# Layer 0 of a two-layer vision state-space model: input projection with 128-row and paired 64-row matmuls, norm sums partly added on GpSimd, residual taken from the gate's tile, new list order

## The chip, the cores and the metric

The kernel runs on one core of a Trainium2 chip. The metric is the device time of one execution in microseconds. Matrix products run on TensorE (PE; PEld is its weight load), elementwise work on VectorE (DVE), ScalarE (ACT) and GpSimd (POOL); every DMA is issued by SyncE (SP). Everything is in fp32.

## What is computed

The input `x` is (4, 128, 128, 192), channels last. Both layers have the form norm, block, residual. The change lies in layer 0, which for each image computes:

- a group norm statistic of x over groups of 6 channels; it is not applied to x but folded into the weights: each row of the projection's weight is multiplied by the channel's inverse deviation, and the mean is turned into a bias.
- `xz = x @ Win.T`: 192 channels to 2 x 384. The first 384 are `xi`, the last 384 the gate `z`.
- `xs = silu(conv3x3(xi) + b)`, depthwise, over 384 channels.
- `x_dbl = x_proj_w @ xs` gives 12 channels for the step size, one row B and one row C; `delta = softplus(dt_w @ dts + dt_b)`.
- a scan over all 16384 pixels, state size 1: `h = exp(delta * A) * h + delta * B * xs`.
- three depthwise 3x3 convolutions of the map of h with dilations 1, 3 and 5, edges replicated, weighted by alpha and summed: `h_f`.
- `y = h_f * C + xs * D`; a layer norm of y over its 384 channels (mean, then the mean of the squared differences); times `silu(z)`; `out = y @ Wout.T`, back to 192 channels.
- residual: `x1 = x + out`, and the norm statistic of x1 for layer 1.

Layer 1 (four scan directions with 16 states, joint processing of image pairs) and the final output follow; the change leaves them as they are.

## The kernel before

Before layer 0, `transpose_in` turns x from pixels-first to channels-first with PE transposes and writes it to a scratch tensor `xT`, as 2 x 96 channels by pixels; on the way it takes the statistics, which `gn_finish` turns into mean and inverse deviation (`gn0`, 96 partitions by two halves).

Layer 0 works on chunks of T = 1024 pixels (R = 8 rows of the picture), NCH = 16 chunks for each of four images, 64 in all. The 384 inner channels are NB = 3 blocks of 128 partitions. For each chunk:

- `load_xa` loads 9 rows of xT into a tile of 96 partitions x 2 halves.
- `project_in` (L392) makes one block of xi: for each half chunk h of 512 pixels it accumulates two matmuls, s = 0 and 1, each with 96 rows of channels. ACT adds the bias and copies to `xi` with a border (L407).
- `conv_in` makes nine products on ACT (L447) and adds eight of them on POOL (L452), then silu (L454); the result xs stays in SBUF and also goes to HBM (`xsd`).
- `project_x` (L471) and `scan`: PE makes the step sizes (L496) and spreads B over partitions (L483), ACT computes softplus and exp (L529, L532), POOL multiplies (L534), DVE multiplies and scans (L537, L539), ACT copies h to a padded tile (L546), POOL fills the pads (L507, L510), SP stores it to HBM (`hpad`).
- one chunk later, `half` for each half chunk: for each block `item` loads shifted copies of h (`sa`, 96 partitions: three rows of taps for 32 channels), runs the dilated taps on PE with diagonal weights (L574), adds eight near taps on DVE (L595), and combines with C, D and xs into y (L605, L606).
- then the layer norm. PE averages over channels with a 128x128 matrix of 1/384 (L633), three accumulating matmuls, one for each block; DVE subtracts (L639), ACT squares (L641), PE averages the squares in the same way (L633), ACT takes log and exp (L644, L646), DVE scales (L653).
- the gate: `xz` is a load of x for these 512 pixels (L648); PE projects it (L660), ACT takes silu (L666), DVE multiplies (L669). PE projects back to 192 channels (L677).
- the residual: x is loaded once more, in two tiles `xr` of 96 partitions (L686), DVE adds PE's result (L688) and takes statistics (L690), SP stores each to `x1T` (L692).

The order of the instructions on each engine is written by a planner in the kernel. The class `Order` collects operations with an engine, a cost, what they read and write, and a due time. `emit` then picks, again and again, the operation that can start first; among those that can start within `idle` of an engine's being free it takes the one of the lowest rank. The rank is the place in the program minus `early`, and an ACT operation that needs another activation table than the one loaded has `keep` added. The result is one fixed list for each engine, SP's DMA issues included: at run time each engine goes through its list in order, and an operation that waits holds up all behind it. A buffer `Buf` has a tag and a number of copies; its next use waits for the last reader of the one before.

Where the weights come from: `scaled(part, b)` scales the projection weights for image b out of a resident tile `win` of both parts on DVE, and computes the bias with small matmuls (L356). Part 0 is xi's, part 1 the gate's; each scaled tile has one copy.

Of the kernel before, what the change touches and what calls it, by code (L numbers as in the profile page):

```python
# [10 lines left out]
F32 = mybir.dt.float32  # L11
# [189 lines left out]
class Maker:  # L201
# [23 lines left out]
    def transpose_in(self, x, xT, gn, ident, p96, eps):  # L225
        nc, tc = self.nc, self.tc
        with tc.tile_pool(name="t_sb", bufs=3) as sb, tc.tile_pool(
            name="t_st", bufs=2
        ) as stp, tc.tile_pool(name="t_ps", bufs=3, space=PSUM) as ps:
            for b in range(B):  # L230
# [26 lines left out]
                self.gn_finish(stp, g, stats, p96, eps, gn[:, b])  # L257

    def layer0(self, xT, x1T, hpad, xsd, gn_in, gn_out, w, ident, p96, eps):
# [8 lines left out]
        with ctx:  # L270
# [6 lines left out]
            win = cp.tile([HC, 2, 6 * 128], F32, name="win")  # L277
            nc.sync.dma_start(win, w["win0"].rearrange("(s c) e -> c s e", s=2))
# [15 lines left out]
            nc.vector.memset(avg, 1.0 / (NB * 128))  # L294

# [30 lines left out]
            od = Order()  # L326
# [13 lines left out]
            def scaled(part, b):  # L340


                t, o = buf(f"w{part}", 1, HC, 2, NB * 128), buf(f"b{part}", 2, 128, NB)
                g = bank2("AC"[part])

                def scale():
                    for s in range(2):
                        nc.vector.tensor_scalar(
                            t()[:, s], win[:, s, part * NB * 128 : (part + 1) * NB * 128],
                            gn_in[:, b, s, 1:2], None, ALU.mult,  # L350
                        )

                def means():
                    for k in range(NB):
                        for s in range(2):
                            nc.tensor.matmul(  # L356
                                g()[:, 0, k : k + 1], t()[:, s, k * 128 : k * 128 + 128],
                                gn_in[:, b, s, 0:1], start=(s == 0), stop=(s == 1),
                            )

                op("DVE", 0.8, scale, writes=[t])
                op("PE", 1.5, means, reads=[t], writes=[g], early=258)
# [6 lines left out]
            def load_xa(b, j):  # L369
# [3 lines left out]
                t = buf("xa", 2, HC, 2, R + 1, W)  # L373
                op("SP", 0.6, lambda: nc.sync.dma_start(
                    t()[:, :, n0 : n0 + hi - lo + 1].rearrange("c s r w -> c s (r w)"),
                    xT[b][:, :, lo * W : (hi + 1) * W].rearrange("s c t -> c s t"),
                ), writes=[t], size=786e3)
                xa[b, j] = t
# [3 lines left out]
            def project_in(b, j, k):  # L382

                x, wt, bt = xa[b, j], wxz[0], bias[0]
# [3 lines left out]
                def mm():  # L388
                    for h in range(2):
# [1272 lines left out]
```

## Time and profile before

Three runs took 26333.76, 26409.49 and 26457.49 us; the median is 26409.49 us.

| | us |
|---|---|
| profiled execution | 26512.26 |
| its span | 26510.5 |
| PE busy | 24193.3 (91%) |
| DVE busy | 21935.4 (83%) |
| ACT busy | 21016.8 (79%) |
| POOL busy | 19902.8 (75%) |
| mean granted TensorE clock | 0.940 |

By stage, the span divides into: transposing in, 0 to 375 us; layer 0, 375 to 6120 us; the input of layer 1, 6120 to 7950 us; its scans, 7950 to 24800 us; the output, 24800 to 26510 us. So layer 0 is 5745 us, 22% of the span, 90 us for each of its 64 chunks.

How to read the lines that follow. Each group of instructions has the line in the kernel, the engine, the operation, what it writes and reads with tile sizes (partitions x elements), the count, and after the bar the busy time in us and the mean in ns; then the idle time of that engine just before these instructions, and what ended it. Busy times of PE are modelled at their ends, since matmuls are pipelined. The clock is the share of full speed that was granted to TensorE. The DMA share is the mean share of time in which the core's 16 DMA engines had a packet; it can go a little above 1 where packets overlap.

### The profile page before, as it was taken

The page shows a single profiled execution, that of the slowest core. Times are in us where ns is not written, and L with a number is a line of the kernel's source. Part 1 is how long each engine was busy: PE and PEld are TensorE (multiplying, and loading weights), DVE is VectorE, ACT ScalarE, POOL GpSimd, SP SyncE. Part 2 cuts the span into 40 slices and gives each one's busy share as a digit, 9 for nine tenths or more (in the row PEclk, how much of TensorE's full clock was granted, in tenths as well). Part 3 has the DMA queues.
Part 4 walks back from the last instruction along what each step waited for, and adds up shares of the span by engine and source line. Part 5 has one row for each costly group of instructions (what it writes and reads, how often), then busy time and mean ns, then how long its engine had stood idle before and what let it go on. Part 6 is the DMA issues. An engine that isn't in the chain of part 4 may idle for free.

```text
span 26510.5 us, 438073 instructions
## 1 busy us (share of the span) xinstructions
PE 24193.3 (91%) x169220; PEld 9017.9 (34%) x169220; DVE 21935.4 (83%) x15401; ACT 21016.8 (79%) x24359; POOL 19902.8 (75%) x9450
## 2 busy tenths in 40 slices
PE   5999999998799999999999999999999999999699
PEld 3333333332233333333333333333333333333255
DVE  4888888888788889989898888888898888988643
ACT  5988898985588888888888888888888888888433
POOL 3777777763488888888888888888888888888400
PEclk7999999998899999999999899999899999999799
DMA  7999999995544444444444444444444444444573
GB/s 213 242 239 241 242 239 241 239 241 182 185 130 127 133 130 136 135 128 125 117 126 134 126 135 130 130 130 130 125 136 131 117 123 115 133 130 130 182 236 105
DMA packets 1667058, 4220.17 MB, mean 159 GB/s; under 512 B 238545, under 2 KB 387473, under 8 KB 1661905
## 3 DMA queue, kind: packets, MB, share of 16 engines
q1 hardware_dynamic: 1664976, 4192.14, 58.0%
q8 instruction: 1340, 21.95, 0.4%
q14 instruction: 742, 6.07, 0.1%
HBM read 3252.11 MB, written 939.10 MB: 158 GB/s over the span
## 4 chain that ended last, share of the span: by engine, by line
PE 40%; DVE 18%; ACT 11%; issue 6%; DMA 4%; POOL 3%; SPq 0%; DVEq 0%; POOLq 0%; ACTq 0%
DVE h L1207 14%; PE f L1174 13%; PE Y L1221 11%; ACT h L1185 6%; PE s L1028 3%; ACT dA L1201 3%; POOL hc L1213 2%; PE s L1051 2%; DMA C<-cs 2%; PE z L785 1%; PE hf L574 1%; DVE D L1100 1%; DVE acc L896 1%; PE f L785 1%; PE s L1094 1%
## 5 line engine op out<-in xcount | busy, mean ns | idle before, releaser
L1213 POOL TENSOR_TENSOR hc<-h,C 128x1024 f32<-128x1024 f32 x6144 | 14335.4, 2362 | 2412.5 <-PE Y L1221 1154.9
L1207 DVE TENSOR_TENSOR_SCAN h<-dA,st,h 128x1024 f32<-128x1024 f32 x5760 | 13130.9, 2331 | 779.9 <-ACT st L1237 290.6
L1185 ACT COPY h<-f 128x1024 f32<-128x1024 f32 (+3 forms) x8192 | 6332.9, 799 | 2256.1 <-PE f L1174 2185.0
L1174 PE MATMUL f<-D,dT 32*64 32x256 f32 x98304 | 7167.9, 408 | 777.5 <-ACT h L1185 633.6
L1221 PE MATMUL Y<-hc,sel 128*64 128x512 f32 x24576 | 7001.5, 657 | 475.1 <-POOL hc L1213 219.9
L1201 ACT ACTIVATE dA<-d,alog 128x1024 f32<-128x1024 f32 x6144 | 6905.9, 1124 | 301.6 <-DVE h L1207 247.2
L1174 PEld LDWEIGHTS f<-D,dT 32*64 32x64 f32 x98304 | 3279.1, 138 | 6688.2 <-ACT h L1185 4815.8
L452 POOL TENSOR_TENSOR xs<-xs,pr 128x1024 f32<-128x1024 f32 x1536 | 3637.3, 2371 | 329.2 <-ACT pr L447 249.4
L595 DVE SCALAR_TENSOR_TENSOR hf<-hh,vec,hf 128x512 f32<-128x512 f32 x3072 | 2317.8, 755 | 412.9 <-PE hf L574 272.7
L1221 PEld LDWEIGHTS Y<-hc,sel 128*64 128x64 f32 x24576 | 1322.6, 141 | 2979.6 <-issue 1811.3
L574 PE MATMUL hf<-sa,diag 96*32 96x512 f32 x18432 | 2152.3, 600 | 13.2 <-DMA sa<-hpad 11.3
L447 ACT ACTIVATE pr<-xi,vec 128x1024 f32<-128x1024 f32 x1536 | 1713.8, 1143 | 301.1 <-POOL xs L452 296.0
L1100 DVE TENSOR_TENSOR D<-s,mask 128x1024 f32<-128x1024 f32 x1024 | 1238.3, 1209 | 842.0 <-PE s L1094 842.0
L534 POOL TENSOR_TENSOR dl<-dl,xs 128x1024 f32<-128x1024 f32 x192 | 454.7, 2368 | 830.6 <-ACT dA L532 735.5
L574 PEld LDWEIGHTS hf<-sa,diag 96*32 96x32 f32 x18432 | 561.9, 109 | 1479.3 <-issue 1390.5
L1061 POOL TENSOR_TENSOR u<-l,u 128x1024 f32<-128x1024 f32 x384 | 907.2, 2363 | 163.4 <-ACT l L1054 136.0
L1207 DVE TENSOR_TENSOR_SCAN h<-dA,h 128x1024 f32<-128x1024 f32 x384 | 857.1, 2274 | 78.5 <-ACT dA L1201 45.3
L1051 PE MATMUL s<-pj,w 128*128 128x512 f32 x1536 | 892.3, 664 | 7.0 <-ACT l L1054 2.8
L1028 PE MATMUL s<-u,w 128*128 128x512 f32 x1536 | 756.4, 630 | 53.3 <-DMA prev<-xc 52.6
L1054 ACT ACTIVATE l<-s,vec 128x512 f32<-128x512 f32 x768 | 527.8, 687 | 328.5 <-PE s L1051 323.9
L1094 PEld LDWEIGHTS s<-ident,pj 128*128 128x128 f32 x4096 | 554.1, 196 | 599.5 <-issue 256.7
L392 PE MATMUL f<-xa,w 96*128 96x512 f32 (+1 forms) x1536 | 724.8, 616 | 25.7 <-ACT xi L407 25.5
(202 smaller groups left out, 21859.5 us busy)
## 6 DMA issues: line engine op xcount, KB each, us to landing
C<-cs SPq DMA_DIRECT2D x4096, 256.0 KB, 4.7
sa<-hpad SPq DMA_DIRECT2D x2304, 276.0 KB, 7.1
d<-delta SPq DMA_DIRECT2D x1536, 256.0 KB, 4.1
u<-xc SPq DMA_DIRECT2D x384, 512.0 KB, 4.6
delta<-l SPq DMA_DIRECT2D x384, 512.0 KB, 3.6
y<-y SPq DMA_DIRECT2D x1536, 128.0 KB, 3.2
hh<-hpad SPq DMA_DIRECT2D x384, 414.0 KB, 7.7
hpad<-hp SPq DMA_DIRECT2D x192, 552.0 KB, 7.2
```

The lines of the kernel that those rows point to most:

```text
L447: op("ACT", 1.1, lambda pr=pr, t=t: nc.scalar.activation(rows(pr()), x()[:, t // 3 : t // 3 + R, t % 3 : t % 3 + W], AF.Copy, scale=v(k, V ...
L452: op("POOL", 2.38, lambda pr=pr: nc.gpsimd.tensor_tensor(o(), o(), pr(), ALU.add), reads=[pr], writes=[o], early=-429)
L574: nc.tensor.matmul(o()[32 * g : 32 * g + 32], diag[:, d, s, k, g], x[:, g, :, c0 : c0 + W], start=(d == 0 and s == 0), stop=(d == 1 and s ...
L595: nc.vector.scalar_tensor_tensor(o3, hh()[:, 1 + dy : 5 + dy, PAD + dx : PAD + dx + W], v(k, V0_K + col), o3, ALU.mult, ALU.add,)
L1028: nc.tensor.matmul(g(), wt()[:, 0, i], uu[i]()[:, 512 * c : 512 * c + 512], start=(i == 0), stop=(i == 2),)
L1100: nc.vector.tensor_tensor(t().rearrange("t a (n s) -> t (a n) s", s=32), g()[:, : 2 * NS].unsqueeze(2).to_broadcast([128, 2 * NS, 32]), ma ...
L1174: nc.tensor.matmul(gs()[64 * jn : 64 * jn + 64, n, 256 * a : 256 * a + 256], td()[rt, r // 64, 2 * sb + a], tD()[rt, a, 256 * jn : 256 * j ...
L1185: nc.scalar.copy(H[:, at : at + nq, 256 * sb : 256 * sb + 256].rearrange("p q (a r s) -> p q a r s", a=2, s=32)[:, :, :, 2 * rp : 2 * rp + 2],
L1201: op("ACT", 1.16, lambda: nc.scalar.activation(a(), d(), AF.Exp, scale=alog[:, c : c + 1]), reads=[d], writes=[a], table="exp", early=-522)
L1207: nc.vector.tensor_tensor_scan(hs[:, way], a()[:, way], hs[:, way], 0.0 if at == 0 else s0()[:, q : q + 1], ALU.mult, ALU.add,)
L1213: op("POOL", 2.4, lambda: nc.gpsimd.tensor_tensor(t(), hs, tC(), ALU.mult), reads=[hq, tC], writes=[t])
L1221: nc.tensor.matmul(ym()[64 * th : 64 * th + 64], sel, t()[:, 512 * th : 512 * th + 512], start=(q == 0), stop=(q == NQ - 1),)
```

## The change

Seven things change, all in layer 0 or just before it:

- The input projection's tile. `load_xa` now loads channels 0 to 127 into `xa` (128 partitions, 9 rows) and channels 128 to 191 into `xb`, whose partitions 0 to 63 hold the first half chunk's rows and partitions 64 to 127 the second's: three DMAs where there was one. `project_in` issues s = 0 for both half chunks with 128 rows, then s = 1 with 64 rows, half 0 in rows 0 to 63 and half 1 in rows 64 to 127.
- For that, part 0 of the weights is laid out with channels 128 to 191 twice. The resident `win` goes; `scaled` loads the raw weights from HBM for every image into the scaled tile and scales them in place.
- The norm's values go to HBM (`gn0d`) at the end of each image of `transpose_in`, and are loaded again as `gn128` in the new layout ahead of layer 0.
- The layer norm's sums. Before each average, POOL adds the three blocks (two adds of 128 x 512), and PE averages the sum with one matmul where there were three.
- The residual is added in the gate's tile `xz`, which gets two copies; the second load of x and the tiles `xr` go. One store writes both halves to `x1T`.
- The planner gets `keep=428, idle=0.150` (before 20 and 0.3) and other values of `early` nearly everywhere in layer 0, so that the fixed lists have another order.
- The costs given to the planner follow: 2.75 for `project_in` (3.6), 0.92 for an average (2.65), 1.22 for an add on POOL.

The diff, without the other changes of `early`:

```diff
-    def transpose_in(self, x, xT, gn, ident, p96, eps):
+    def transpose_in(self, x, xT, gn, gnd, ident, p96, eps):
...
                 self.gn_finish(stp, g, stats, p96, eps, gn[:, b])
+                nc.sync.dma_start(gnd[b].rearrange("(s c) v -> c s v", s=2), gn[:, b])
...
-            win = cp.tile([HC, 2, 6 * 128], F32, name="win")
-            nc.sync.dma_start(win, w["win0"].rearrange("(s c) e -> c s e", s=2))
...
+            gn128 = cp.tile([128, B, 2, 2], F32, name="gn128")
+            for b in range(B):
+                nc.sync.dma_start(gn128[:, b, 0], gnd[b][:128])
+                for q in range(2):
+                    nc.sync.dma_start(gn128[64 * q : 64 * q + 64, b, 1], gnd[b][128:])
...
-            od = Order()
+            od = Order(keep=428, idle=0.150)
...
+                if part:
+                    t = buf("w1", 1, HC, 2, NB * 128)
+                    gn = [(slice(0, HC), gn_in[:, b, s]) for s in range(2)]
+                    rows_ = [(slice(0, HC), s, src[s * HC : (s + 1) * HC]) for s in range(2)]
+                else:
+                    t = buf("w0", 1, 128, 2, NB * 128)
+                    gn = [(slice(0, 128), gn128[:, b, 0]), (slice(0, 128), gn128[:, b, 1])]
+                    rows_ = [
+                        (slice(0, 128), 0, src[:128]),
+                        (slice(0, 64), 1, src[128:]),
+                        (slice(64, 128), 1, src[128:]),
+                    ]
+
+                def load():
+                    for p, s, x in rows_:
+                        nc.sync.dma_start(t()[p, s], x)
...
+                op("SP", 0.5, load, writes=[t], size=295e3, early=75)
...
-                t = buf("xa", 2, HC, 2, R + 1, W)
-                op("SP", 0.6, lambda: nc.sync.dma_start(
-                    t()[:, :, n0 : n0 + hi - lo + 1].rearrange("c s r w -> c s (r w)"),
-                    xT[b][:, :, lo * W : (hi + 1) * W].rearrange("s c t -> c s t"),
-                ), writes=[t], size=786e3)
+                t, t2 = buf("xa", 2, 128, R + 1, W), buf("xb", 2, 128, 5, W)
+                x = xT[b].rearrange("s c t -> (s c) t")
+
+                def load():
+                    for p, ch, at, n, r in (
+                        (slice(0, 128), slice(0, 128), n0, hi - lo + 1, lo),
+                        (slice(0, 64), slice(128, C), n0, 5 - n0, lo),
+                        (slice(64, 128), slice(128, C), 1, hi - R * j - 4, R * j + 5),
+                    ):
...
                 def mm():
-                    for h in range(2):
-                        m = min(4, n - 4 * h)
-                        for s in range(2):
+                    for s in range(2):
+                        for h in range(2):
+                            m = min(4, n - 4 * h)
+                            p = slice(64 * h, 64 * h + 64) if s else slice(0, 128)
                             nc.tensor.matmul(
-                                g()[:, h, : m * W], wt()[:, s, k * 128 : k * 128 + 128],
-                                x()[:, s, 1 + 4 * h : 1 + 4 * h + m],
+                                g()[:, h, : m * W], wt()[p, s, k * 128 : k * 128 + 128],
+                                x2()[p, 1 : 1 + m] if s else x()[:, 1 + 4 * h : 1 + 4 * h + m],
                                 start=(s == 0), stop=(s == 1),
                             )
...
-                op("PE", 3.6, mm, reads=[x, wt], writes=[g, t], early=219)
-                op("POOL", 0.3, edges, writes=[t])
-                op("ACT", 1.12, copy, reads=[g, bt], writes=[t], early=-657)
+                op("PE", 2.75, mm, reads=[x, x2, wt], writes=[g, t], early=-48)
+                op("POOL", 0.3, edges, writes=[t], early=2409)
+                op("ACT", 1.12, copy, reads=[g, bt], writes=[t], early=-21)
...
-                gm, gv, xz = bank(), bank(), buf("xz", 1, HC, 2, 512)
+                gm, gv, xz = bank(), bank(), buf("xz", 2, HC, 2, 512)
+                ysum = buf("ys", 1, 128, 512)
...
                 def average(out, src):
-                    for k in range(NB):
-                        nc.tensor.matmul(
-                            out(), avg, src[k](), start=(k == 0), stop=(k == NB - 1)
-                        )
-
-                op("PE", 2.65, lambda: average(gm, ys), reads=ys, writes=[gm], early=-411)
+                    nc.tensor.matmul(out(), avg, src(), start=True, stop=True)
+
+                def add(out, a, b):
+                    op("POOL", 1.22, lambda: nc.gpsimd.tensor_tensor(out(), a(), b(), ALU.add),
+                       reads=[a, b], writes=[out])
+
+                add(ysum, ys[0], ys[1])
+                add(ysum, ysum, ys[2])
+                op("PE", 0.92, lambda: average(gm, ysum), reads=[ysum], writes=[gm])
...
-                op("PE", 2.65, lambda: average(gv, sq), reads=sq, writes=[gv], early=-411)
+                add(sq[0], sq[0], sq[1])
+                add(sq[0], sq[0], sq[2])
+                op("PE", 0.92, lambda: average(gv, sq[0]), reads=[sq[0]], writes=[gv])
...
-                    xr = buf(f"xr{s}", 1, HC, 512)
-                    op("SP", 0.4, lambda s=s, xr=xr: nc.sync.dma_start(
-                        xr(), xT[b][s, :, c1 : c1 + 512]), writes=[xr], size=197e3)
-                    op("DVE", 0.68, lambda s=s, xr=xr: nc.vector.tensor_tensor(
-                        xr(), xr(), g()[:HC, s], ALU.add), reads=[g], writes=[xr])
+                    op("DVE", 0.68, lambda s=s: nc.vector.tensor_tensor(
+                        xz()[:, s], xz()[:, s], g()[:HC, s], ALU.add), reads=[g], writes=[xz], early=-120)
...
-                    op("SP", 0.4, lambda s=s, xr=xr: nc.sync.dma_start(
-                        x1T[b][s * HC : (s + 1) * HC, c1 : c1 + 512], xr()
-                    ), reads=[xr], size=197e3)
+                op("SP", 0.4, lambda: nc.sync.dma_start(
+                    x1T[b][:, c1 : c1 + 512].rearrange("(s c) t -> c s t", s=2), xz()
+                ), reads=[xz], size=393e3)
```

## The prediction

> **What bounds the kernel now.** The edit touches layer 0, the short work before it, and nothing later. I therefore read first the busy time by stage (columns: window, its length, then busy us and instruction counts of PE, PE weight loads, DVE, ACT, POOL; granted clock; DMA share; GB/s).
>
> ```profile
> 375.00:570.00 195.00, 103.31 (x228) 38.68 (x232) 26.57 (x27) 155.01 (x162) 172.98 (x105) 0.61 0.31 90
> 570.00:5870.00 5300.00, 5263.00 (x26004) 1761.30 (x26000) 4375.11 (x5636) 4741.76 (x5161) 3988.07 (x2407) 0.99 0.97 240
> 5870.00:6120.00 250.00, 223.34 (x1072) 75.93 (x1064) 204.25 (x290) 79.77 (x97) 5.58 (x7) 0.96 0.84 194
> 7950.00:24800.00 16850.00, 15457.62 (x127108) 5705.83 (x127108) 14994.32 (x7823) 14034.81 (x16809) 14526.42 (x6234) 0.94 0.47 128
> ```
>
> Layer 0 is a fill of 195 us, a body of 5300 us and a tail of 250 us. In the body TensorE is busy 5263 of 5300 us, 99.3%, at clock 0.99: it sets the time. The others are close behind: DMA share 0.97, ACT 89%, DVE 83%, POOL 75%. The last row is the scan stage of layer 1, where no engine is full: its best is PE with 91.7%.
>
> Second, the groups of instructions inside layer 0, to see what PE's time is made of and where POOL's gaps are.
>
> ```profile
> L452 POOL TENSOR_TENSOR xs<-xs,pr 128x1024 f32<-128x1024 f32 x1536 | 3637.3, 2371 | 329.2 <-ACT pr L447 249.4 <-DMA sa<-hpad 0.7
> L392 PE MATMUL f<-xa,w 96*128 96x512 f32 (+1 forms) x1536 | 724.8, 616 | 25.7 <-ACT xi L407 25.5 <-DMA xa<-xT 0.2
> L534 POOL TENSOR_TENSOR dl<-dl,xs 128x1024 f32<-128x1024 f32 x192 | 454.7, 2368 | 830.6 <-ACT dA L532 735.5 <-ACT state L544 82.0 <-DMA sa<-hpad 7.1
> L633 PE MATMUL g<-sq,avg 128*128 128x512 f32 x768 | 362.9, 608 | 0.0
> L633 PE MATMUL g<-y,avg 128*128 128x512 f32 x768 | 361.8, 607 | 0.0
> L510 POOL COPY hp<-hp 128x40 f32<-128x40 f32 x192 | 42.6, 222 | 0.1
> ```
>
> A matmul statement is two instructions here (192 calls with four statements give x1536 on L392). The two averages (L633) cost PE 725 us and the input projection (L392) 725 us. POOL's largest gap is the 736 us that it stands before L534 until ACT's dA is there.
>
> Third, a stretch of the timeline, for the price of one matmul (start, length, engine, line, operation, tile rows*columns; in brackets the idle time before).
>
> ```profile
> 3002.14 0.19 PEld L660 LDWEIGHTS g<-xz,w 96*128 96x128 f32 x1 [0.24 <-issue]
> 3003.09 0.16 PEld L574 LDWEIGHTS hf<-sa,diag 96*32 96x32 f32 x8 [0.76 <-issue]
> 3003.09 2.79 PE L574 MATMUL hf<-sa,diag 96*32 96x512 f32 x24
> ...
> 3005.81 1.12 PE L483 MATMUL g<-proj,ident 32*128 32x512 f32 x2
> ...
> 3006.86 2.84 PE L633 MATMUL g<-y,avg 128*128 128x512 f32 x6
> ...
> 3009.63 2.79 PE L574 MATMUL hf<-sa,diag 96*32 96x512 f32 x24
> ...
> 3017.68 1.13 PE L483 MATMUL f<-proj,ident 32*128 32x512 f32 x4
> ...
> 3018.74 2.84 PE L633 MATMUL g<-sq,avg 128*128 128x512 f32 x6
> ```
>
> Weight loads inside a group follow each other every 0.43 us (0.19 plus the 0.24 of idle): that is the price of one 512-column instruction, whether it has 96 or 128 rows. From 3006.86 to 3009.63, six instructions take 2.77 us: 6 x 0.43 and 0.19 more, because the next group has another tile shape. The L483 rows tell the second thing: two instructions in one 32-row tile take 1.05 us (3005.81 to 3006.86), and four in two different 32-row tiles take 1.06 us (3017.68 to 3018.74). Tiles of different rows run side by side.
>
> **The change, part by part.** The sum is made against the profiled execution, 26512.3 us (span 26510.5); that run lies 0.4% above the median of 26409.5, and I subtract the same microseconds from the median.
>
> *Averages.* Per half chunk, two groups go from six instructions to two. 4 x 0.43 = 1.72 us, 256 groups: 440 us off PE.
>
> *Input projection.* Per call 128 rows for two statements, and two statements of 64 rows in different tiles, writing two banks. If the 64-row pair runs side by side as the 32-row pair does, eight steps become six: 2 x 0.43 x 192 = 165 us off PE. No 64-row pair is in this trace; the bounds are 0 (they queue) and 165, and I take 165, since L483's pair overlaps fully (1.06 against 1.05).
>
> *Tile shapes.* The rule that speaks against this part: the row has 0.76 us of idle before the first weight load of a new shape instead of 0.24, and the group then ends 0.14 to 0.19 us late. The Trainium skill, "TensorEngine Tiling (Array Packing)", section Key Properties, says that a change of tiling mode (not of tile) drains the array. A full drain would be the tail of a matmul (592 ns long at a pitch of 430, so 0.16) and a bare weight load (0.19), 0.35 us. Counting shape changes in layer 0's list of matmuls gives 1460 before and 1894 after: 434 more, 74 us by the row (0.17 each), 152 by the full drain. I take 74.
>
> PE in sum: -440 - 165 + 74 = -531 us. By the share of these instructions in the body (L633 has 94% of its there) some 502 of it are there: 5263 - 502 = 4761.
>
> *GpSimd adds.* 512 adds of 128x512. From L452 (1024 elements, 2371 ns) and L510 (40 elements, 222 ns) the slope is 2.18 ns an element, so 222 + 472 x 2.18 = 1.25 us; half of L452 would be 1.19. At 1.22: 625 us, 610 of it in the body. POOL goes from 3988 to 4598. Nothing on POOL hides this: it is the gaps of POOL that must take it. An add that waits for DVE's y holds the convolution adds queued behind it, and for those ACT's products wait (three buffers). PE's average now waits for POOL; queued behind it on PE are the dilated taps, and DVE's taps wait for these.
>
> *List order.* In the new list ACT's table loads in layer 0 fall from 949 to 801; at the 1283 ns of each such row in this trace that is 190 us off ACT: 4742 to 4552. No ACT, DVE or PE operation is otherwise added or dropped. DVE stays at 4375: the residual add and its statistics keep their sizes.
>
> *Residual from the gate's tile.* 256 reloads of 192 KB disappear, 256 stores become 128 of twice the size, 64 input loads become 192 smaller ones, 20 weight loads and 16 tiny ones for the norm come in. SP issues 221 fewer DMAs, some 0.33 us each; it waits for buffers most of the time, so this is worth nothing. Of the bytes, 256 x 197 KB = 50 MB of about 1340 (233 GB/s x 5745 us) go, 3.8%. DMA time in the body: 5300 x 0.97 = 5141, less 3.8%: about 4941. A share of 1.0 isn't the ceiling, since windows of 100 us inside the body show 1.05 (1770 to 1870 us).
>
> *Weights reloaded per image.* The load waits for the last matmul on the old weights, and SP's later loads are queued behind it. SP's longest such waits on PE now are 9 us; six later loads: 0 to 55 us, hidden as long as the two-deep tap tiles are full. I take 0.
>
> *Before layer 0.* The store of the norm's values stands on SP ahead of the next image's loads. Now the next load is issued at 88.52 while the value is ready at 93.83; PE then waits for that load until 97.54. So 5.3 us at each of three image changes, 16 us. Then 12 small loads (0.45 us each) come before the first weights: 5.4 us, and about 2 more for the norm's trip through HBM. Sum +23 us (10 to 40), uncovered.
>
> *What the body then takes.* Demand, in us: DMA 4941 of share, PE 4761, POOL 4598, ACT 4552, DVE 4375. Five resources within 12%; before, PE was alone. Lower end: PE as full as now, 4761/0.993 = 4795. Upper end: PE only as full as in the scan stage, where several engines are near each other, 4761/0.917 = 5192. I take the middle, 4990: PE 95%, POOL 92%, ACT 91%, DMA 0.99. The tail is left as it is (PE loses 10 us, the chain gains as much through the adds).
>
> Here a second rule bears: a PE that idles more may be clocked down. Rows: 5870 to 5970 has PE 95.8% busy at clock 1.00, 1970 to 2070 97.9% at 0.93, and the scan stage 91.7% at 0.94. The Trainium skill, "TensorE: Matmul & The Clock Gate", Part 1, says that the clock halves after an idle window of about 3.4 us and comes back after as much busy time. By the rows 95% busy needs cost nothing; by the page, gaps over 3.4 us would cost the following 3.4 us half its speed. At the scan stage's 0.94 PE's demand would be 4761 x 0.99/0.94 = 5014, and the body at least that. I take the rows; this end lies inside the upper one.
>
> Sum: -310 + 23 = -287 us. 26512 - 287 = 26225 for a profiled run; 26409 - 287 = 26122 for the median.
>
> **Rivals.**
> 1. *DMA becomes the bound.* For: share 0.97 at 240 GB/s already. Against: SP waits over 1000 us for PE to free tap tiles, so the queue isn't what is short, and 1.05 occurs. At today's share: 4941/0.97 = 5094, -206 + 23: 26226.
> 2. *PE stays the bound and is as full as now.* For: it is 99.3% full today, so every other wait is absorbed. Against: POOL would be 96% full and now stands between two of PE's groups. 4795: -505 + 23: 25928.
> 3. *The 64-row pair doesn't overlap* (the change doesn't do what it says). The projection then saves nothing and pays the switches: PE 4761 + 156 = 4917, at 95.4% a body of 5154: -146 + 23: 26286. Against it stands the L483 pair.
> 4. *POOL becomes the bound (slower).* In the body POOL stands still 5300 - 3988 = 1312 us, much of it waiting for ACT in a fixed list. It must lose 610 of these. If its waits are latencies that remain, the body is 4598 + 1312 = 5910 and the time 27040. The change pays nothing once POOL's idle time in the body stays above 5300 - 4598 = 702 us; at 900 it gives 5498, +221, 26630. Against it: most of the 736 us before L534 is POOL being early while PE sets the pace.
>
> **How the numbers follow.** Main case (25990 to 26220) 0.45; DMA 0.22; PE full 0.15; no overlap 0.06; POOL slower 0.12. 0.5% of the median is 132 us, about what a measurement can tell: faster is below 26277. Faster: 0.43 + 0.19 + 0.15 + 0.03 = 0.80. Same: 0.02 + 0.03 + 0.03 + 0.03 = 0.11. Slower: 0.09. The range leaves out most of rival 4 above and, below, the end of rival 2 with a full body and no start cost: 25880 to 26400.
>
> **What would show it.** Right: the average's group at x512 instead of x1536, the projection's calls at about 2.8 us, POOL adds near 1.2 us, PE below 98% and POOL above 88% in the body, DMA share about 0.99. Wrong: 64-row matmuls starting only after one another; POOL with over 700 us of idle in the body, before its own new adds; DVE or PE waiting for DMA by hundreds of us; a clock in the body below 0.96.

## The result, and the profile after

The changed kernel takes 26062.93 us (median of four runs, 26017.38 to 26093.08); the kernel before, run beside it on the same chip, takes 26433.49 us (26333.76 to 26474.52). The ratio is 0.9869, with a 95% interval of 0.984 to 0.9897: 1.3% faster. 26122 was predicted, with 25880 to 26400 as the range. A second measurement of the same kernel later, beside other runs, gave 0.9888 (0.9853 to 0.9923).

The profiled executions took 26512.26 us before and 26079.12 us after, 433 us apart. Layer 0 ends 292 us earlier (its norm is stored at 6117.2 us before, at 5825.2 after; -287 was predicted). The other 141 us lie in stages whose code is the same in both, above all the scans of layer 1 (17541 us before, 17425 after, from the first to the last of their projection matmuls). Over the 14 profiles of this study that stage lies between 17341 and 17541 us with no relation to what was changed, while layer 0 of the changed kernel repeats within some 10 us. So I compare layer 0, and use whole times for the sign and for what is larger than that spread.

The changed kernel's busy time by stage; the columns are those of the same view shown above: window, its length, busy us and counts of PE, weight loads, DVE, ACT and POOL, then clock, DMA share and GB/s.

```profile
386.00:585.00 199.00, 97.18 (x240) 30.87 (x240) 26.08 (x29) 152.21 (x159) 171.73 (x103) 0.62 0.29 87
585.00:5595.00 5010.00, 4863.54 (x25058) 1493.15 (x25058) 4395.15 (x5652) 4539.06 (x5027) 4588.31 (x2898) 0.98 0.97 246
5595.00:5828.00 233.00, 194.11 (x976) 60.91 (x974) 192.83 (x273) 69.41 (x85) 33.76 (x29) 0.91 0.80 187
7659.00:24509.00 16850.00, 15410.68 (x127713) 5701.08 (x127710) 15077.74 (x7881) 14121.86 (x16878) 14618.12 (x6268) 0.95 0.47 129
```

The body went from 5300 to 5010 us. PE is busy 4863.54 of 5010 us, 97.1%; POOL has gone from 75% to 91.6%, ACT is at 90.6%, DVE at 87.7%, DMA still at 0.97. PE is still the fullest engine.

Counted from the first tap of the dilated convolutions to the last convolution add, the body went from 5281.4 to 4992.3 us: -289.1. The start came 17.8 us later (first copy of xi at 406.0 instead of 388.2 us), the fill between the two took 3.3 us less, the tail 17.5 us less. -289.1 + 17.8 - 3.3 - 17.5 = -292.1.

The groups of layer 0 in the changed kernel; after the bar busy us and mean ns, then the engine's idle time just before them and what ended it:

```profile
L493 POOL TENSOR_TENSOR xs<-xs,pr 128x1024 f32<-128x1024 f32 x1536 | 3640.4, 2372 | 251.8 <-ACT pr L488 185.7 <-ACT state L585 3.6
L615 PE MATMUL hf<-sa,diag 96*32 96x512 f32 x18432 | 2191.8, 614 | 78.5 <-DVE y L646 43.6 <-issue 15.3 <-DMA sa<-hpad 13.8
L575 POOL TENSOR_TENSOR dl<-dl,xs 128x1024 f32<-128x1024 f32 x192 | 455.1, 2370 | 33.5 <-ACT dA L573 29.6 <-DMA sa<-hpad 3.2
L431 PE MATMUL f<-xa,w 128*128 128x512 f32 (+1 forms) x768 | 396.1, 640 | 32.3 <-issue 12.5 <-ACT xi L446 10.9 <-DVE dA L580 8.5
L676 POOL TENSOR_TENSOR sq<-sq,sq 128x512 f32<-128x512 f32 x256 | 328.3, 1283 | 71.4 <-ACT sq L685 61.3
L431 PE MATMUL f<-xb,w 64*128 64x512 f32 (+1 forms) x768 | 222.0, 652 | 0.0
L673 PE MATMUL g<-sq,avg 128*128 128x512 f32 x256 | 148.8, 664 | 20.0 <-POOL sq L676 19.9
L673 PE MATMUL g<-ys,avg 128*128 128x512 f32 x256 | 145.9, 653 | 13.3 <-POOL ys L676 9.9 <-DMA sa<-hpad 3.1
```

The averages (L673, before L633) fell from 724.7 to 294.7 us, the projection (L431, before L392) from 724.8 to 618.1. One add of POOL (L676) takes 1283 ns. POOL's 735.5 us before the product of step size and xs (L575, before L534) have shrunk to 29.6.

A projection call on PE's timeline (start, length, engine, line, operation, tile rows*columns, count):

```profile
2987.62 2.79 PE L615 MATMUL hf<-sa,diag 96*32 96x512 f32 x24
2990.34 1.98 PE L431 MATMUL f<-xa,w 128*128 128x512 f32 x4
2992.26 1.13 PE L431 MATMUL f<-xb,w 64*128 64x512 f32 x4
2993.31 5.39 PE L723 MATMUL f<-y,wout 128*96 128x512 f32 x12
2998.54 1.02 PE L673 MATMUL g<-ys,avg 128*128 128x512 f32 x2
```

Four instructions of 128 rows take 1.92 us from start to start. The four of 64 rows, two in the upper and two in the lower half of the array, take 1.05 us together: as long as two, so the pair runs side by side. The call lasts from 2990.34 to 2993.31, 2.97 us.

### The profile page after: what moved, and what is told of

Read it like the earlier page. It is cut to its first block, busy times and chain, and to the rows that moved or that the text cites. A ratio compares the mean times of both kernels' runs of the same rounds, so it can differ in the third digit from the quotient of the medians.

```text
span 26077.3 us, 435537 instructions
## 1 busy us (share of the span) xinstructions
PE 23595.6 (90%) x168196; PEld 8682.5 (33%) x168196; DVE 21939.2 (84%) x15401; ACT 20827.2 (80%) x24211; POOL 20540.0 (79%) x9962
## 4 chain that ended last, share of the span: by engine, by line
PE 47%; DVE 21%; ACT 13%; issue 7%; DMA 6%; POOL 5%; SPq 1%; DVEq 0%; POOLq 0%; ACTq 0%
DVE h L1250 14%; PE f L1217 13%; PE Y L1264 10%; ACT h L1228 6%; PE hf L615 5%; ACT dA L1244 3%; PE s L1071 3%; POOL hc L1256 2%; PE s L1094 2%; POOL xs L493 2%; PE g L706 2%; PE f L723 2%; DVE hf L635 2%; PE z L828 1%; DMA C<-cs 1%
## 5 line engine op out<-in xcount | busy, mean ns | idle before, releaser
L1217 PE MATMUL f<-D,dT 32*64 32x256 f32 x98304 | 7087.0, 404 | 795.8 <-ACT h L1228 649.7
L1264 PE MATMUL Y<-hc,sel 128*64 128x512 f32 x24576 | 6928.0, 651 | 479.9 <-POOL hc L1256 223.6
L493 POOL TENSOR_TENSOR xs<-xs,pr 128x1024 f32<-128x1024 f32 x1536 | 3640.4, 2372 | 251.8 <-ACT pr L488 185.7
L615 PE MATMUL hf<-sa,diag 96*32 96x512 f32 x18432 | 2191.8, 614 | 78.5 <-DVE y L646 43.6
L706 PE MATMUL g<-xz,w 96*128 96x512 f32 x1536 | 769.1, 626 | 28.6 <-DVE y L699 14.8
L939 DVE SCALAR_TENSOR_TENSOR acc<-xi,vec,acc 128x1024 f32<-128x1024 f32 x384 | 715.0, 1862 | 26.8
```

The source lines that it names most:

```text
L493: op("POOL", 2.38, lambda pr=pr: nc.gpsimd.tensor_tensor(o(), o(), pr(), ALU.add), reads=[pr], writes=[o], early=-390)
L615: nc.tensor.matmul(o()[32 * g : 32 * g + 32], diag[:, d, s, k, g], x[:, g, :, c0 : c0 + W], start=(d == 0 and s == 0), stop=(d == 1 and s ...
L1217: nc.tensor.matmul(gs()[64 * jn : 64 * jn + 64, n, 256 * a : 256 * a + 256], td()[rt, r // 64, 2 * sb + a], tD()[rt, a, 256 * jn : 256 * j ...
L1264: nc.tensor.matmul(ym()[64 * th : 64 * th + 64], sel, t()[:, 512 * th : 512 * th + 512], start=(q == 0), stop=(q == NQ - 1),)
```

## The experiments

The theory to test was that of the prediction: PE sets the pace of the body before and after, so the work taken off PE is what pays, and the list is in the background. Its rivals: POOL or the DMA has become the bound; the 64-row pair does not overlap; the gain is the list's. All experiments change the kernels in layer 0 or its start alone. "Body" is counted in each as above, from the first dilated tap to the last convolution add.

### The new operations with the old list's numbers

All operations of the changed kernel are kept; the planner gets the `keep`, `idle` and `early` of before.

```diff
-            od = Order(keep=428, idle=0.150)
+            od = Order()
...
-                op("PE", 2.75, mm, reads=[x, x2, wt], writes=[g, t], early=-48)
+                op("PE", 2.75, mm, reads=[x, x2, wt], writes=[g, t], early=219)
...
```

> The changed kernel's operations, with the planner's old numbers (keep 20, idle 0.3, every old value of early; the POOL adds get the averages' old -411). ACT table loads rise again. My theory (PE's shorter work sets the time, the order only lets it through): layer 0, which took 5729 us before and 5419 us after the change, takes 5480 to 5600, and the run is faster than the kernel before by 0.5 to 1.0%. Rival A (the new order is what pays): layer 0 at 5680 or more, the run within 0.3% of before. Rival B (POOL is the bound in any order): 5419 to 5450, no loss against the changed kernel.

Measured: ratio 0.9994 (0.9975 to 1.0013), the time of before. The body takes 5286.7 us. With some 420 us of averages and the projection's saving off PE, the body is as long as before. The expectation missed: layer 0 takes 5703 us, where rival A put it (5680 or more).

Busy time in the body (same columns as above):

```profile
590.00:5856.00 5266.00, 4928.91 (x24937) 1532.11 (x24932) 4368.89 (x5627) 4596.60 (x5058) 4580.68 (x2890) 0.95 0.92 233
```

The same view of the changed kernel:

```profile
590.00:5560.00 4970.00, 4828.35 (x24876) 1482.54 (x24874) 4361.50 (x5611) 4513.22 (x4998) 4570.99 (x2886) 0.98 0.97 246
```

The same instructions, within a few at the window's ends. PE stands idle 337 us (5266.00 - 4928.91) instead of 142: 195 of the 296 us. Its matmuls are also dearer, 197.7 ns of busy time per instruction against 194.1, which is some 89 us, at a clock of 0.95 against 0.98. Changes of tile shape don't make them dearer: the body has 1672 of them here and 1820 in the changed kernel (96 and 128 rows or columns taken as one shape). The rest, 12 us, is the few more instructions in the window.

What PE waited for between 590 and 5500 us with the old numbers (sum in us, times, longest; behind "issue" stands a wait whose cause the profile doesn't show):

```profile
PE hf L615 <- DVE y L646: 70.6, 33, 5.5
PE hf L615 <- issue: 56.7, 19, 5.0
PE g L673 <- POOL sq L676: 43.4, 15, 6.4
PE g L706 <- DVE y L699: 40.9, 28, 4.3
```

And in the changed kernel:

```profile
PE hf L615 <- DVE y L646: 35.5, 38, 2.2
...
PE g L706 <- DVE y L699: 13.4, 18, 1.9
PE hf L615 <- issue: 12.9, 7, 2.4
PE g L673 <- POOL sq L676: 11.9, 14, 3.7
```

These four make up 211.6 us of 318.6 with the old numbers and 73.7 of 144.3 in the changed kernel. Over the whole of both lists PE waits 177 times instead of 136, and 1.8 us on average instead of 1.1: more often, and above all longer.

### The old operations with the new list's numbers

The kernel before, with `Order(keep=428, idle=0.150)` and the new `early` of every operation that both kernels have.

> The kernel before with only the planner's new numbers (keep 428, idle 0.150, the new values of early). My theory: PE is 99.3% full in the body of layer 0 whatever the list, so fewer ACT table loads buy nothing: layer 0 5700 to 5800 us, the run within 0.4% of before, perhaps slower. Rival A (the order pays): layer 0 below 5600, faster by 0.5% or more.

Measured: ratio 1.0027 (1.0011 to 1.0043), body 5404.1 us, 123 us longer than before; layer 0 takes 5858 us, beyond the 5800 expected. So the new numbers are no better in themselves: on the old operations they are worse than the old ones.

| body, us | old numbers | new numbers |
|---|---|---|
| old operations | 5281.4 | 5404.1 |
| new operations | 5286.7 | 4992.3 |

Neither half pays alone. The gain of 289 us belongs to the pair.

### Which part of the numbers

First the new `keep` and `idle` with the old `early`, then the reverse, both with the new operations.

```diff
-            od = Order()
+            od = Order(keep=428, idle=0.150)
```

> The changed kernel's operations, the planner's keep and idle as changed (428, 0.150), every early as before. With the old numbers throughout, these operations gave a body of layer 0 (first dilated taps to last convolution add) of 5287 us; the changed kernel gives 4992, the kernel before 5281. ACT loads 825 tables (old numbers 851, changed 801). My theory now (the due times decide whether PE finds ready work; keep and idle only trim ACT): body 5200 to 5290. Rival (grouping of tables and the narrower idle carry it): body below 5100.

> The changed kernel with only keep and idle put back (20, 0.3), 841 table loads. My theory (due times carry it): body 5000 to 5100, most of the gain stays. Rival (keep and idle carry it): body above 5200. If both this run and its counterpart lie above 5200, the numbers work only together.

Measured: `keep` and `idle` alone give a body of 5176.3 us (ratio 0.9973, 0.996 to 0.9985); `early` alone gives 5289.5 us (ratio 0.9978, 0.9967 to 0.999). Of the 294 us between the old and the new numbers, `keep` and `idle` bring 110, `early` alone nothing, and both together all. That `early` carries it is refuted; that `keep` and `idle` carry it holds for somewhat more than a third. Busy time in the body, first `keep` and `idle` alone:

```profile
590.00:5748.00 5158.00, 4882.31 (x24749) 1515.80 (x24746) 4328.19 (x5580) 4533.60 (x5013) 4568.85 (x2881) 0.95 0.94 236
```

Then `early` alone:

```profile
590.00:5860.00 5270.00, 4956.11 (x24976) 1524.01 (x24972) 4385.55 (x5647) 4574.62 (x5048) 4576.77 (x2890) 0.95 0.93 233
```

`keep` is the penalty for a change of ACT's table, so ACT's table loads in layer 0 were the obvious mechanism: 949 before, 801 in the changed kernel. They don't explain it: old numbers 851, `keep` and `idle` alone 825, `early` alone 841, whose bodies are 5287, 5176 and 5290.

### Do the old numbers suffer from POOL's adds, or from the averages?

On top of the new operations with old numbers: once all adds but the first cut to 32 of 512 columns, once the old three-matmul averages in place of the adds.

> The changed kernel's operations with all the planner's old numbers (body 5287 us), and three of four POOL adds of each half chunk cut to 32 columns, so the norm's sums are incomplete. Lists as in that run. If the old list fails because POOL's new work comes late (415 us less of it): body 5000 to 5150. If it fails because its due times suit another set of operations, whatever POOL's load: body above 5220.

> All the planner's old numbers, the averages as before with three matmuls and no POOL adds; of the changed kernel the paired projection, the residual from the gate's tile and the reloaded weights remain. PE has 100 us less to do than before (165 less, 66 for tile shapes). If the POOL adds are what the old numbers can't place: body 5180 to 5230 against 5281 before. If any change of the operations spoils the old numbers: 5270 or more.

One run each; the first leaves the norm's sums incomplete, so only its time is of use. The bodies are 5273.2 and 5283.9 us. Taking 363 us off POOL (4580.68 to 4218.17 between 590 and 5856 us) moves the body by 13 us; so with the old numbers POOL's load isn't what holds it. With the averages back on PE only the projection with its reloaded weights and the residual differ from before:

```profile
590.00:5920.00 5330.00, 5197.64 (x26008) 1690.45 (x26004) 4395.99 (x5657) 4695.11 (x5138) 3995.90 (x2414) 0.99 0.92 231
```

PE is 97.5% full here, where it was 99.3% before. The projection's saving turns into PE's idle time. So the projection's saving is lost on the old numbers even without the adds, and the wait of the averages for POOL cannot be the only cause.

### PE's work: the averages three times

The average issues its matmul three times on the same sum, so that PE has the work of before while everything else stays as in the changed kernel.

```diff
-                    nc.tensor.matmul(out(), avg, src(), start=True, stop=True)
+                    for _ in range(3):
+                        nc.tensor.matmul(out(), avg, src(), start=True, stop=True)
```

> The changed kernel with every average's one matmul issued three times on the same sum, with the planner's costs left as they are: each engine's list is unchanged but for the repeats, and the POOL adds stay. PE gets back 512 x 0.86 = 440 us, some 415 of it in the body. My theory (PE, 97% full in the body, is still what sets the time): layer 0 longer by 280 to 400 us. Rival B (POOL, 92% full, sets it and PE has slack): longer by less than 200 us.

Measured: ratio 0.9966 (0.9951 to 0.9982). The averages cost 734 us instead of 295, +439; the body grows by 290.9 us, to 5283.2, and layer 0 by 310 (280 to 400 were expected). PE fills up again:

```profile
590.00:5857.00 5267.00, 5176.99 (x25844) 1657.60 (x25846) 4374.44 (x5616) 4523.97 (x5004) 4579.60 (x2889) 0.99 0.91 232
```

98.3% and a clock of 0.99. Two thirds of the added work shows in the time. Of the rest, 52 us go into PE's idle time (142 to 90 in these windows), and others into cheaper matmuls elsewhere. The 291 us are the whole gain: with the averages' work back on PE the body is as long as before the change (5281.4), although the projection still costs PE 107 us less. The dilated taps' group in this run:

```profile
L615 PE MATMUL hf<-sa,diag 96*32 96x512 f32 x18432 | 2152.8, 605 | 50.5 <-DVE y L646 20.6 <-issue 13.2 <-DMA sa<-hpad 12.2
```

2152.8 us for the same 18432 instructions that take 2191.8 in the changed kernel, 2218.7 with the old numbers, and 2152.3 before. With the list and the tile shapes of the changed kernel, a fuller PE does this group 39 us faster.

The whole run is nevertheless 81 us shorter than that of before (medians), although its layer 0 ends 24 us later (at 6141.7 against 6117.2 us). `early` alone is a second such case: 62 us shorter as a whole, 8 by the end of layer 0. As far as the profiles show, these differences lie in stages that no run here changes, and nothing here explains them; so I go by layer 0.

### POOL's work: adds of 32 columns

The adds of the changed kernel, except the first, work on 32 columns. The norm's sums are then incomplete; only the time is of use.

```diff
-                def add(out, a, b):
+                def add(out, a, b, n=32):
...
-                add(ysum, ys[0], ys[1])
+                add(ysum, ys[0], ys[1], 512)
```

> The changed kernel with three of the four POOL adds of each half chunk cut to 32 of 512 columns, so the norm's sums are incomplete; lists and waits unchanged. POOL loses 384 x about 1.08 us = 415 us. My theory (PE sets the time): PE had 2.8% of the body idle, 140 us, part of it waiting for these adds, so layer 0 gets shorter by 20 to 100 us. Rival B (POOL sets the time): shorter by 250 us or more.

Measured: ratio 0.9846 (0.9822 to 0.9871), body 4971.0 us, 21 us shorter than the changed kernel's, layer 0 30 us shorter. Its adds of squares:

```profile
L676 POOL TENSOR_TENSOR sq<-sq,sq 128x32 f32<-128x32 f32 x256 | 64.4, 251 | 152.2 <-ACT sq L686 147.3 <-ACT state L585 1.6
```

An add falls from 1283 to 251 ns, which takes POOL from 4571 to 4206 us in the body's window. 365 us off POOL give 21 us. POOL is 92% full, and is not the bound.

### The 64-row pair: half chunks one after the other

The two loops of the projection are exchanged, so that each 64-row matmul stands between two of 128 rows and its partner cannot run beside it.

```diff
-                    for s in range(2):
-                        for h in range(2):
+                    for h in range(2):
+                        for s in range(2):
```

> The changed kernel with the four statements of the input projection in the order half 0 (128 rows, 64 rows), half 1 (128 rows, 64 rows): the two 64-row statements no longer stand side by side, and the tile shape changes two more times a call. Lists and planner otherwise unchanged. If the pair overlaps in the changed kernel (my theory), PE gets 0.86 + 2 x 0.17 = 1.2 us more for each of 192 calls, 230 us, and layer 0 is longer by 120 to 230 us. If the pair didn't overlap anyway, only the switches come in: 65 us, at most 70 longer.

Measured: ratio 0.9939 (0.992 to 0.9959), body 5156.0 us, +164; layer 0 +163.5.

```profile
L431 PE MATMUL f<-xb,w 64*128 64x512 f32 (+1 forms) x768 | 459.3, 680 | 0.0
...
L431 PE MATMUL f<-xa,w 128*128 128x512 f32 (+1 forms) x768 | 453.0, 673 | 22.0 <-issue 11.4 <-DVE dA L580 9.0 <-ACT xi L446 1.5
```

The projection takes 912 us instead of 618. A stretch of its timeline (start, length) shows why:

```profile
3056.07 1.12 PE L431 MATMUL f<-xa,w 128*128 128x512 f32 x2
3057.12 1.12 PE L431 MATMUL f<-xb,w 64*128 64x512 f32 x2
3058.18 1.12 PE L431 MATMUL f<-xa,w 128*128 128x512 f32 x2
```

Each pair of instructions now takes 1.05 us instead of 2 x 0.43: the overlap is gone, and each change of tile shape adds 0.19. The pair's overlap and grouping together are worth 164 us of time. The 912 us are also more than the old projection cost (725 us): without the grouping, this part of the change would add work to PE.

### The DMA: the second load of x again

The two loads of x for the residual come back, into tiles that nobody reads: 50 MB more.

```diff
+                    for s in range(2):
+                        nc.sync.dma_start(xr[s](), xT[b][s, :, c1 : c1 + 512])
```

> The changed kernel with the two reloads of x (192 KB each) issued again beside the gate's load, into tiles that nothing reads; lists and waits otherwise unchanged. 50 MB more, about 200 us of the 16 DMA engines' time. My theory (DMA, at a share of 0.97 in the body, has room up to about 1.05): layer 0 longer by 0 to 70 us. Rival (DMA is the next bound): longer by 130 to 200 us.

Measured: body 4999.1 us, +7; layer 0 +6.

```profile
590.00:5570.00 4980.00, 4814.52 (x24880) 1479.44 (x24884) 4362.44 (x5615) 4510.16 (x5001) 4571.56 (x2887) 0.98 1.01 255
```

The DMA share rises from 0.97 to 1.01, the rate from 246 to 255 GB/s, and PE does not notice. The whole time, 26171.75 us (ratio 0.9906, 0.9886 to 0.9926), is higher than the changed kernel's, but that difference isn't in layer 0. So the second load's removal is worth at most some 7 us in this layer, and the DMA isn't the bound.

### The changed kernel again

> The changed kernel once more, for the spread between executions. Layer 0 (first copy of xi to the store of its norm) 5419 us, its body 4992; both again within 20 us. The scan stage of layer 1, whose code is the same in all runs, lay between 17341 and 17541 us in ten profiles, so it may differ by 100 us.

Measured: 26110.69 us, ratio 0.9888 (0.9853 to 0.9923), body 4987.0 us (4992.3 in the first profile). Layer 0 repeats to 10 us.

### A shorter start

The store of the norm's values is issued by ACT's queue, and the values come back in three loads from one scratch tensor instead of twelve.

```diff
-                nc.sync.dma_start(gnd[b].rearrange("(s c) v -> c s v", s=2), gn[:, b])
+                nc.scalar.dma_start(gnd[b].rearrange("(s c) v -> c s v", s=2), gn[:, b])
...
+            gall = gnd.rearrange("b c v -> c b v")
+            nc.scalar.dma_start(gn128[:, :, 0], gall[:128])
+            for q in range(2):
+                nc.scalar.dma_start(gn128[64 * q : 64 * q + 64, :, 1], gall[128:])
```

> The changed kernel with the norm's small stores and loads issued by ACT instead of SP, the loads of all four images in three DMAs instead of twelve. In the changed kernel the first copy of xi starts at 406.0 us, before the change at 388.2. My theory (SP's queue made that difference: 5 us at each of three image changes while the store waits, 5 us of small loads): first copy at 387 to 394, layer 0 as in the changed kernel within 20 us. Rival (the trip of the values through HBM and the new weight loads made it): 400 or later.

Measured: 26033.79 us, ratio 0.9857 (0.9824 to 0.989). The change from the first to the second image, before the change (SPq and ACTq are the issue of a DMA):

```profile
88.52 6.68 SPq L234 DMA_DIRECT2D xin<-in_x  x3
...
97.54 0.84 PE L243 MATMUL pt<-ident,xin 128*96 128x128 f32 x3 [4.20 <-DMA xin<-in_x]
```

In the changed kernel:

```profile
94.01 0.30 SPq L258 DMA_DIRECT2D gn<-gn  x1
94.41 5.62 SPq L234 DMA_DIRECT2D xin<-in_x  x3
...
103.59 0.63 PE L243 MATMUL pt<-ident,xin 128*96 128x128 f32 x2 [10.10 <-DMA xin<-in_x]
```

And with the shorter start:

```profile
90.50 5.93 SPq L234 DMA_DIRECT2D xin<-in_x  x3
95.85 0.36 ACTq L258 DMA_DIRECT2D gn0d<-gn  x1
98.82 1.49 PE L243 MATMUL pt<-ident,xin 128*96 128x128 f32 x6 [3.49 <-DMA xin<-in_x]
```

In the changed kernel the next image's loads stand behind the store; here they don't, and PE resumes 4.8 us earlier. The first copy of xi comes at 393.5 us instead of 406.0, inside the 387 to 394 expected, and layer 0 ends at 5802.0 instead of 5825.2, the earliest of all versions that compute the whole sums. Its whole time can't be told from the changed kernel's (the intervals overlap).

## Why the prediction was right, and where it was not

**The total.** -287 us was predicted against the profiled execution's own time, and layer 0 ends 292 us earlier. The median moved by 371 us against the runs beside it, 60 us below the 26122 predicted, well inside the range; the difference is of the size by which the untouched stages differ from run to run. That -287 and -292 lie so close is partly luck: the body gave 289 us where 310 were forecast, and the tail, which the prediction left as it was, gave 17.5.

**PE's sum: -531 predicted, -435 measured** (5589.65 to 5154.83 in layer 0). The averages gave 430 of 440. The projection and the shape changes were set at -165 + 74 = -91; the projection with its own changes measured -107. What was missed is that other groups got dearer: the taps by 40 us, the gate's projection by 42. The run with the averages three times has the same list and shapes but a fuller PE, and there the taps cost what they did before (2152.8) and the gate's projection 751.9. So of the 82 us, 56 come and go with how full PE is, that is with its clock (below); the remaining 25 of the gate's projection fit the shape changes, which no run isolates. The size of the shape term holds: 0.19 us a change in the exchanged loops, 0.17 was taken.

**The clock: the row was the wrong choice.** "By the rows 95% busy needs cost nothing" does not hold. Over these runs the body's clock falls where PE is less full: 99.3% (before) 0.99, 98.3% (averages three times) 0.99, 97.1% (changed) 0.98, 94.7% and 93.6% (other numbers) 0.95. With the same instructions 93.6% against 97.1% made them about 89 us dearer. Fullness alone doesn't set it: the run with the loops exchanged is 98.2% full at 0.98, the old numbers with averages on PE 97.5% at 0.99.

The traces' clock records show what is behind these means. The clock has two levels, 1.0 and 0.5, and each stretch at 0.5 lasts a multiple of 3.41 us. In the body before, 14 such stretches took 88 us, in the changed kernel 28 took 258, with the old numbers 79 took 513, with the averages three times 18 took 139. Most follow a wait of PE. One in the changed kernel (same columns as the other tables of busy time):

```profile
4436.00:4456.00 20.00, 17.34 (x99) 5.05 (x97) 16.29 (x24) 19.83 (x22) 17.04 (x12) 1.00 1.04 272
4456.00:4476.00 20.00, 20.00 (x64) 5.15 (x66) 13.60 (x16) 13.30 (x14) 12.06 (x8) 0.50 0.98 231
4477.00:4497.00 20.00, 20.00 (x104) 6.58 (x100) 17.72 (x23) 17.28 (x21) 15.88 (x9) 1.00 1.01 277
```

The wait just before it is this one:

```profile
4454.92 1.13 PE L537 MATMUL f<-proj,dtw 32*128 32x512 f32 x4 [1.78 <-ACT xi L446]
```

After 1.78 us of waiting PE runs at half clock for 20 us, busy all the time. The Trainium skill, "TensorE: Matmul & The Clock Gate", Part 1, from which I had taken that only gaps over some 3.4 us cost speed, agrees with the two levels and the step; but the body of the changed kernel has 8 waits over 3.4 us and 28 stretches at half clock, so shorter waits cost too. An estimate from these stretches, which halve the speed: the clock can have cost the changed kernel at most half of 258 - 88, some 85 us, more than the kernel before (the two groups named above got 82 us dearer), and given back at most half of 258 - 139, some 60 us, with the averages three times (56). What decides that a wait of a given length lowers the clock, and for how long, stays open.

**PE's fullness: 95% predicted, 97.1% measured.** This offset the dearer matmuls: 4761/0.95 and 4864/0.971 give the same body of 5010 us. The body's 4990 was right by luck: two terms missed in opposite directions.

**The list: the step that failed, in a total that came out right.** The prediction took the new list for "190 us off ACT" and nothing else. ACT did fall as said (4742 to 4539 in the body, 801 table loads), but that isn't what the list is for. With the old numbers the same operations give 5287 us, with the new ones 4992. The forecast of a middle between "PE as full as now" and "only as full as in the scan stage" is in truth a forecast of how well the list fits, and I had read nothing in the profile before that could say it. The old-numbers kernel, less its 89 us of dearer matmuls, would be at 5198, near the upper end that I had set (5192), which may be chance: that end stood for less work on a PE only 91.7% full.

What stays open is which places in the new list spare PE its long waits. The time is spread over many small ones, and neither table loads nor POOL's load nor `early` alone accounts for them. I did not find the one order that decides.

**POOL: right.** 1.22 us was taken for an add, 1283 ns measured: 657 us in all instead of 625. POOL is 91.6% full (92% predicted), with 422 us of idle time in the body, below the 702 from which rival 4 would decide. Its 736 us before the step-size product were being early, as argued against that rival: 30 are left, and 285 us now lie before its adds, which wait for DVE's y (224) or ACT's squares (61). The adds cut to 32 columns settle it.

**The DMA: right in sum.** The share is 0.97 (0.99 predicted), since the transfers took 5143 - 4847 = 296 us of share less, not 200; why they took so much less is open. Rival 1 falls with the second load.

**The pair: right.** Rival 3 falls. The run with the loops exchanged is what it would have looked like: its body of 5156 us meets the 5154 worked out for the rival, though by luck, with other terms: more work on PE (+216 us in the body's window, not +156) and a fuller PE (98.2%, not 95.4%).

**The start: +23 predicted, +17.8 measured.** The store in front of the next image's loads is there: PE resumes at 103.59 us where it resumed at 97.54, 6 us for the 5.3 taken. Removing store and small loads from SP takes 12.5 us of the 17.8 back.

**Rival 2** (PE as full as before, body 4795) did not come: 97.1%, not 99.3%.

## What to carry to other kernels

Taking work off the engine that sets the time may pay only once the fixed order of the instructions is fitted to the new work: here the same operations gave nothing under the old order's numbers and 289 us of 5281 under new ones, and the new numbers cost 123 us on the old operations. So judge an edit and its order together, and after an edit that "should" pay and doesn't, look at the idle time of the engine that was full before giving up the edit. Half-height matmuls were worth their change of tile shape here only where the partners in the other rows stood directly behind each other (618 us for the projection, against 912).

## What the runs showed of the hardware

- A change of tile shape had a steady price. A pair of fp32 matmul instructions of 512 columns takes 0.86 us among its like and 1.05 us at a change (1.05 to 1.06 from start to start in the run with the loops exchanged). 64 rows against 128 rows pay it as 32 against 96 did before.
- TensorE's granted clock reacts to a few per cent of idle time: mostly 0.98 to 0.99 at 97 to 98% busy, 0.95 at 93.6 to 94.7%. The lower means are made of stretches at half clock, one of them 20 us after a wait of 1.78 us. An idle PE thus costs more than its idle time: the old numbers' 195 us more of idle came with some 89 us of dearer matmuls.
- An add of two fp32 tiles on GpSimd took 251 ns for 128x32, 1283 ns for 128x512 and 2372 ns for 128x1024: 2.15 ns an element between the first two and 2.13 between the last two.
- The 16 DMA engines went from 246 to 255 GB/s at a share of 1.01 when asked to. A share of 0.97 was not their limit.
